# Four-layer image network on one core: the last image's activations kept in SBUF, its offset work split by halves, and two rules of the instruction planner changed

## The chip, the core and the metric

One NeuronCore of a Trainium2 chip runs the whole program in one launch. Its engines are TensorE (PE, with weight loads as PEld), VectorE (DVE), ScalarE (ACT), GpSimd (POOL) and the DMA queues, of which SyncE (SP) issues most. The metric is the device time of the launch in microseconds; lower is better. Every number below is from one core.

## What is computed

Four images of 96 channels by 64 x 64 pixels (`B, C, H, W = 4, 96, 64, 64`, so `L = 4096` positions) pass through four residual layers. All numbers are float32 except inside the two feed-forward parts, which round to 8 and 16 bits.

```python
x = x + L0(group_norm(x))            # a selective scan in four directions
x = x + L1(group_norm(x))            # a deformable 3x3 convolution
t = tokens(x)                        # L tokens of 96 channels
t = t + fourier(layer_norm(t))       # 192 hidden channels, DFT along the tokens and back
t = t + ffn2(layer_norm(t))
t = t + linear_attention(layer_norm(t))
t = t + ffn3(layer_norm(t))
```

Layer 0 projects each pixel to 192 channels, convolves, and then runs `h = exp(d*A)*h + d*u*B` over the 4096 positions, for 192 channels with 16 states each, along rows, columns, and both reversed; the four results are summed, normed over channels, gated by `z` and projected back to 96 channels. Layer 1 computes from the normed image 18 offsets and 9 masks per pixel by a 3x3 convolution, fetches for each of the 9 taps four neighbouring pixels at the shifted place, weighs them bilinearly, and multiplies by a 96 x 96 matrix per tap. The rest works on tokens.

## The kernel before

The Python code writes instructions in one order per engine, and each engine runs its own list in that order, waiting on semaphores. What stands where in those lists is settled when the program is built, by a small planner.

**The scan is the backbone.** `Layer0.scan` (L900) makes 1536 units: per image 4 directions, 4 time steps of 1024 positions, 3 groups of 64 channels, 8 units each. A unit is a decay on ACT (L1016), two products on PE that spread `d*u` (L1022), a product on DVE (L1036), the scan itself on DVE (L1044), a product on POOL (L1053) and sums on PE (L1072). Its tiles come from the pool `l0s`: twelve buffers of tag `da` (128 x 1024) and two of tag `bc` (128 x 2 x 1024). ACT's queue issues the `da` loads, SP's the others.

**Two streams fill in beside it.** `ends()` makes the inputs of the scan for images 0 to 3 (`first`, `before`) and then runs layers 2 and 3 of images 0, 1, 2, 3 one after the other (`Layers23.image`). `middle()` runs for each image `Layer0.behind` (sum of directions, norm, gate, projection: `x1`, L1094) and `Layer1.image` (L1223: `offsets`, `positions`, `sample`: `x2`). A stream is a generator that yields, after each few instructions, a `Step` with the time that they are taken to need on each engine. `Clock` adds these up. `pipe` (L272) keeps several chains of one kind open at once and picks the first whose tokens (`takes`, `frees`) and PSUM banks are free and that `Clock.has_room` lets in. `Stream.step` does the same for a stream. `has_bank` (L403) limits the PSUM banks that chains hold over a step to three; after the scan the stream `ends` gets five banks of its own.

**Who goes first.** After each scan unit `go()` lets every stream place one step, `middle` ahead of `ends`; from the moment the last image is being sampled, `ends` is asked first. After the scan the function `alone()` does the same without units.

**Layer 1 of an image.** `offsets` (L1242) loads `x1` from DRAM, takes the group norm's statistics (`bn_stats`, L448), norms `x` in place on ACT (L1262) and copies it with POOL into a padded tile (L1264). Then eight chunks of 512 positions follow: the 3x3 convolution on PE (L1280), its bias on ACT (L1291), four transposes of pixels (L1297), a copy to `pix` (L1299), the fold of the four partial sums (L1302), and eight DMAs per chunk that write the pixels four times into the gather table in DRAM (L1312, 64 in all). `positions` (L1317) loads the constant `base` and computes on DVE, for all 32 blocks of 128 pixels at once, the index and the four weights of each tap. Its tiles lie where those of `offsets` lay. `sample` (L1368) has 32 blocks x 3 chains: three indirect DMAs from POOL (L1385), the weighing, transposes on PE (L1418), and for each pair of blocks nine products with the weights (L1434), after which `x1` is loaded from DRAM, added (L1439), and stored as `x2` (L1441). During the scan ACT does the weighing (L1397), after it DVE (L1404 to L1406).

**Layers 2 and 3 of an image.** `Layers23.image` waits until `x2` of the image is complete, loads it (L1827), norms all of it (`normed`, L1605), and runs the Fourier part in two halves of channels: `hidden` (L1553), first DFT (L1512), twiddle (L1578), inverse (L1512), last (L1592, L1597). For the last image the rest is done in two halves of tokens side by side.

Of the kernel before, what the change touches and what calls it, by code (L numbers as in the profile page):

```python
# [8 lines left out]
F32 = mybir.dt.float32  # L9
# [11 lines left out]
L = H * W  # L21
# [250 lines left out]
def pipe(net, chains, width, every=0, lane=None, **tiles):  # L272
# [5 lines left out]
    while True:  # L278
# [9 lines left out]
        for n, chain in enumerate(active):  # L288
            if chain.new and not net.has_bank():
                continue  # L290
# [6 lines left out]
            if not all(free[tag] > 0 for tag in chain.takes):  # L297
                continue
# [5 lines left out]
        for tag in chain.takes:  # L304
            free[tag] -= 1
# [54 lines left out]
class Net:  # L360
# [3 lines left out]
    def __init__(self, ctx, tc, ins):  # L364
# [20 lines left out]
        self.sampling_last = False  # L385
        self.clock, self.known, self.streams, self.stream = Clock(), {}, [], None
# [16 lines left out]
    def has_bank(self):  # L403
        if self.own_banks:
            return self.stream.held < (5 if self.stream.own else 3)
        return sum(stream.held for stream in self.streams) < 3
# [36 lines left out]
    def group_norm_stats(self, x, pool, key, stats):  # L443

        nc = self.nc
        st = pool.tile([C, NCH, 6], F32, name=f"gnst{key}", tag="gnst")
        for j in range(NCH):
            nc.vector.bn_stats(st[:, j, :], x[:, j * CH : (j + 1) * CH])  # L448
            if j % 2:
                yield cost(dve=1.4)  # L450
# [22 lines left out]
    def centred(self, x, cen, dst, key, pool, bias=None, groups=(0, 1)):  # L473
# [7 lines left out]
        def chain(j):  # L481
            yield wait(new=True, takes="sq")
# [72 lines left out]
class Layer0:  # L555
# [440 lines left out]

    def fetch_step(self, u):

        u.bc = self.sp.tile([128, 2, T], F32, name=f"bc{u.key}", tag="bc")
        for s in range(2):  # L1000
            src = self.bc_d[u.b][u.k][NS * s : NS * s + NS, u.ts]
            self.net.nc.sync.dma_start(u.bc[:, s, :], src.unsqueeze(1).to_broadcast([NS, D8, T]))
# [91 lines left out]
    def behind(self, b):  # L1094
# [6 lines left out]
        with (  # L1101
# [3 lines left out]
            cen_a, cen_c, wo_a, wo_c = (net.load(q, big) for q in ("cen_a", "cen_c", "wo_a", "wo_c"))  # L1105
            for j0 in range(NCH - HB, -1, -HB):
                if j0 % (NCH // 2) == NCH // 2 - HB:

                    h0 = H // 2 * (j0 * 2 // NCH)
                    yta = big.tile([128, W, H // 2], F32, name=f"yta{b}_{h0}", tag="yta")  # L1110
                    ytc = big.tile([D2, W, H // 2], F32, name=f"ytc{b}_{h0}", tag="ytc")
                    for yt, c0 in ((yta, 0), (ytc, 128)):
                        src = self.y_d[b][3][c0 : c0 + yt.shape[0]].rearrange("c (w h) -> c w h", h=H)
                        nc.sync.dma_start(yt, src[:, :, h0 : h0 + H // 2])
                    yta_v, ytc_v = (t.rearrange("p w h -> p h w") for t in (yta, ytc))
                    yield wait(4.0)
                while not all((b, 2, j * CH // T) in self.summed for j in range(j0, j0 + HB)):
                    yield BLOCKED
                ca = big.tile([128, HB, CH], F32, name=f"ca{b}_{j0}", tag="ca")
# [5 lines left out]
                def centred(i):  # L1125
# [8 lines left out]
                    for y, yt in ((ya, yta_v), (yc, ytc_v)):  # L1134
                        y = y.rearrange("p (h w) -> p h w", w=W)
                        nc.gpsimd.tensor_add(y, y, yt[:, rs, :])
                    yield cost(pool=3.1, new=True)
# [22 lines left out]
                nw = op.tile([128, CH], F32, name=f"nw{b}_{j0}", tag="nw", bufs=1)  # L1160
# [3 lines left out]
                def gated(i):  # L1164
# [16 lines left out]
                    for o, n, z, vg, vb in parts:  # L1181
                        nc.gpsimd.tensor_mul(o[:, i, :], o[:, i, :], z)
                    xr = op.tile([C, CH], F32, name=f"xr{b}_{j}", tag="xr")
                    nc.sync.dma_start(xr, ins["x"][b][:, cs])
                    yield cost(pool=2.6, new=True)
# [6 lines left out]
                    yield cost(dve=0.7)  # L1192
                    nc.sync.dma_start(self.x1[b][:, cs], xr)
                    yield NOTHING

                yield from pipe(self.net, (gated(i) for i in range(HB)), 2)


class Layer1:
# [23 lines left out]
    def image(self, b):  # L1223
        tc = self.net.tc
        with tc.tile_pool(name=f"l1i{b}", bufs=1, side="right") as ix:
            idx = ix.tile([128, 288], U32, name=f"idx{b}", tag="idx")
            wt = ix.tile([128, 288, 4], F32, name=f"wt{b}", tag="wt")
            yield from self.before(b, idx, wt)
            self.net.sampling_last = b == B - 1
            yield from self.sample(b, idx, wt)  # L1230
        self.net.sampled.add(b)

    def before(self, b, idx, wt):
# [3 lines left out]
        with tc.tile_pool(name=f"l1o{b}", bufs=1, side="right") as keep:  # L1237
            om = keep.tile([128, 32, 27], F32, name=f"om{b}", tag="om")
            yield from self.offsets(b, om)
            yield from self.positions(b, om, idx, wt)  # L1240

    def offsets(self, b, om):  # L1242

        net = self.net
        tc, nc = net.tc, net.nc
        with tc.tile_pool(name=f"l1a{b}", bufs=1, side="right") as pre:
            x = pre.tile([C, L], F32, name=f"x1_{b}", tag="x")
            nc.sync.dma_start(x, self.x1[b])
# [4 lines left out]
            yield wait(4.0)  # L1253
            stats = []
            yield from net.group_norm_stats(x, pre, f"1_{b}", stats)
# [3 lines left out]
            yield cost(dve=0.2)  # L1259
            def filled(j):  # L1260
                cs = slice(j * CH, (j + 1) * CH)
                nc.scalar.activation(x[:, cs], x[:, cs], AF.Identity, scale=rstd, bias=nmr)  # L1262
                yield cost(act=0.8)
                nc.gpsimd.tensor_copy(  # L1264
                    pad[:, 1 + j * NR : 1 + (j + 1) * NR, 1 : 1 + W],
                    x[:, cs].rearrange("p (h w) -> p h w", w=W),
# [676 lines left out]
```

## Time and profile before

| what | value |
|---|---|
| median of 3 runs | 8444.11 us (8442.93 to 8499.31) |
| the profiled execution's own time | 8460.68 us |
| its span, first to last instruction | 8458.9 us |
| busy: PE, DVE, POOL, ACT | 76%, 80%, 66%, 59% of the span |
| first and last scan on DVE start at | 189.2 us, 7407.8 us |
| DMA | 1608.26 MB, 190 GB/s over the span |
| mean granted PE clock | 0.793 of full |

The profile is of one execution, 16.6 us above the median of the runs; the span is the time from the first to the last instruction. The page divides the span into 40 slices of 211 us and gives each engine's busy share in tenths. "Granted clock" is the share of full speed that PE's clock had. An answer by windows gives, for each stretch, its length, then the busy time and the number of instructions of each engine, then the granted clock, the DMA engines' share and what they moved in GB/s. The chain of waits follows the work that ended last back to what released it. fp32 products show as two rows of the profile for one instruction of the program. The table below puts names to the stretches after the last scan.

| us from the start | what ends each stretch |
|---|---|
| 7411 to 7472 | `x1` of the last image complete |
| 7472 to 7523 | first product of its offset convolution |
| 7523 to 7578 | last write of its gather table |
| 7578 to 7607 | first transposes of gathered pixels |
| 7607 to 8041 | last chunk of `x2` |
| 8041 to 8082 | first product of its Fourier part |
| 8082 to 8459 | end |

### The profile page before, as it was taken

What the parts mean: (1) busy time and instruction counts of PE and PEld (TensorE: products, weight loads), DVE (VectorE), ACT (ScalarE), POOL (GpSimd) and SP (SyncE); (2) the same over time, 40 slices, a digit from 0 to 9 for tenths busy, and PEclk for the clock granted to TensorE, in tenths of its full rate; (3) what the DMA queues carried; (4) which work ended last, traced back from release to release, by engine and by line L of the source; (5) the groups of instructions that cost most, each with busy time, mean ns of one, the idle gap of its engine ahead of it and who ended that gap; (6) DMA issues with size and microseconds to landing.
All of it is one profiled execution on the core that took longest, in us unless ns stands there. A gap on an engine that the chain in (4) does not pass through costs nothing.

```text
span 8458.9 us, 96090 instructions
## 1 busy us (share of the span) xinstructions
PE 6423.3 (76%) x31810; PEld 2788.5 (33%) x31848; DVE 6748.3 (80%) x5122; ACT 5005.0 (59%) x9171; POOL 5580.3 (66%) x4308
## 2 busy tenths in 40 slices
PE   6776777679767776877667788877688867788687
PEld 2211221112222233321122366422265522365373
DVE  2699989987688998778899889798988889827714
ACT  5665566646467787755577666454566775423224
POOL 0466556665468888756588888676788887617700
PEclk9776786778667777977778788877789878888798
DMA  3687778977678998877789899876899988745420
GB/s 92 162 217 200 170 190 223 227 177 188 152 210 233 236 244 224 214 168 190 201 236 246 224 236 235 195 177 165 218 236 232 235 206 192 169 103 159 145 61 16
DMA packets 773925, 1608.26 MB, mean 190 GB/s; under 512 B 264081, under 2 KB 355757, under 8 KB 771222
## 3 DMA queue, kind: packets, MB, share of 16 engines
q10 hardware_dynamic: 244224, 843.17, 39.7%
q1 hardware_dynamic: 455478, 532.37, 24.2%
q0 software_dynamic: 73728, 226.57, 10.1%
q8 instruction: 256, 4.19, 0.2%
q14 instruction: 239, 1.96, 0.1%
HBM read 1345.43 MB, written 256.29 MB: 189 GB/s over the span
## 4 chain that ended last, share of the span: by engine, by line
PE 32%; DVE 28%; DMA 11%; POOL 10%; ACT 9%; issue 8%; ACTq 1%; SPq 1%; DVEq 0%; another core or an unknown queue 0%; POOLq 0%
DVE da L1044 13%; POOL da L1053 7%; DVE db L1036 7%; PE pc L763 4%; PE ps L1418 3%; PE py L1072 3%; PE f L1512 3%; ACT g L1397 2%; PE pd L1434 2%; PE db L1022 2%; ACT da L1016 2%; POOL g L1385 2%; DMA da<-de 1%; DMA du<-du 1%; PE h L1553 1%
## 5 line engine op out<-in xcount | busy, mean ns | idle before, releaser
L1053 POOL TENSOR_TENSOR da<-da,bc 128x1024 f32<-128x1024 f32 x1536 | 3636.1, 2369 | 286.4 <-DVE da L1044 166.4
L1044 DVE TENSOR_TENSOR_SCAN da<-da,st,db 128x1024 f32<-128x1024 f32 x1152 | 2700.6, 2344 | 115.6 <-ACT da L1016 5.2
L1036 DVE TENSOR_TENSOR db<-db,bc 128x1024 f32<-128x1024 f32 x1536 | 1865.6, 1215 | 647.8 <-PE db L1022 646.2
L1016 ACT ACTIVATE da<-da,w_al 128x1024 f32<-128x1024 f32 x1536 | 1739.4, 1146 | 384.0 <-DMA da<-de 148.3
L1385 POOL DMA_INDIRECT g<-table,idx x1152 | 1199.8, 1042 | 378.2 <-issue 177.0
L1022 PE MATMUL db<-du,rep 24*128 24x512 bf16 x3072 | 690.5, 454 | 804.0 <-DVE da L1044 763.7
L1072 PE MATMUL py<-da,w_fold 128*32 128x512 f32 x6144 | 1076.7, 774 | 24.0 <-POOL da L1053 11.8
L1397 ACT ACTIVATE g<-g,wt 128x96 f32<-128x96 f32 x3456 | 969.4, 365 | 80.9 <-PE py L1072 19.8
L1044 DVE TENSOR_TENSOR_SCAN da<-da,db 128x1024 f32<-128x1024 f32 x384 | 877.2, 2284 | 58.0 <-ACT da L1016 21.9
L1418 PE MATMUL ps<-w_ident,g 128*96 128x128 f32 x3744 | 678.6, 331 | 205.0 <-issue 51.1
L1022 PEld LDWEIGHTS <-rep 24*128 24x128 bf16 x3072 | 148.6, 93 | 1929.7 <-DVE da L1044 1188.0
L850 POOL TENSOR_TENSOR lw<-lw,w 128x512 f32<-128x512 f32 x192 | 244.1, 1271 | 678.1 <-DVE w L848 634.8
L1051 POOL COPY st<-da 128x1 f32<-128x1 f32 x1152 | 228.7, 199 | 696.0 <-DVE da L1044 666.2
L1418 PEld LDWEIGHTS ps<-w_ident,g 128*96 128x96 f32 x3744 | 502.1, 149 | 532.0 <-ACT g L1397 151.2
L763 PE MATMUL pc<-pad,wc 96*128 96x512 f32 x1152 | 579.2, 640 | 13.5 <-DMA wc<-wc_d 4.1
L1426 ACT COPY st<-ps 96x384 f32<-96x384 f32 x384 | 180.4, 473 | 530.4 <-PE ps L1418 483.4
L884 PE MATMUL pr<-ex,w_ident 128*128 128x512 f32 x384 | 295.4, 861 | 71.0 <-DVE ex L864 19.4
L840 PE MATMUL pd<-xd,w_dtw 103*64 103x512 f32 (+1 forms) x512 | 270.1, 798 | 81.6 <-DMA w_dtw<-in_dtw 29.7
L763 PEld LDWEIGHTS pc<-pad,wc 96*128 96x128 f32 x1152 | 218.3, 200 | 313.1 <-issue 284.5
L1434 PE MATMUL pd<-st,wdc 96*128 96x256 f32 x1152 | 313.2, 421 | 3.2 <-ACT zt L789 1.8
L886 ACT CAST du<-pr 128x512 bf16<-128x512 f32 x192 | 111.6, 581 | 275.2 <-PE pr L885 190.1
L1521 ACT COPY d<-f 128x512 f32<-128x512 f32 x192 | 111.6, 583 | 273.3 <-PE f L1512 272.9
(260 smaller groups left out, 8860.8 us busy)
## 6 DMA issues: line engine op xcount, KB each, us to landing
da<-de ACTq DMA_DIRECT2D x1536, 512.0 KB
du<-du SPq DMA_DIRECT2D x1536, 96.0 KB
bc<-bcd SPq DMA_DIRECT2D x128, 512.0 KB
y<-yb SPq DMA_DIRECT2D x384, 128.0 KB
de<-rl SPq DMA_DIRECT2D x128, 256.0 KB
m<-in_dft SPq DMA_DIRECT2D x128, 256.0 KB
ad<-y ACTq DMA_DIRECT2D x192, 128.0 KB
table<-pix SPq DMA_DIRECT2D x256, 96.0 KB
```

The costliest lines, as they stand in the source:

```text
L763: nc.tensor.matmul(pp, lhsT=wc[:, q, g * 128 : (g + 1) * 128], rhs=pad[:, r0 + dy : r0 + dy + NR, dx : dx + W], start=(q == 0), stop=(q == 8),
L884: nc.tensor.matmul(pr, lhsT=net.ident, rhs=ex, start=True, stop=False)
L1016: self.net.nc.scalar.activation(u.da, u.da, AF.Exp, scale=self.al[:, a : a + 1])
L1022: self.net.nc.tensor.matmul(db[:, h, :], lhsT=self.rep[64 * u.q + 32 * h : 64 * u.q + 32 * h + 24], rhs=u.du[64 * u.q + 32 * h : 64 * u.q ...
L1036: self.net.nc.vector.tensor_mul(u.db, u.db, u.bc[:, 0, :])
L1044: nc.vector.tensor_tensor_scan(u.along(u.hh), u.along(u.da), u.along(u.db), first, ALU.mult, ALU.add)
L1053: self.net.nc.gpsimd.tensor_mul(u.hh, u.hh, u.bc[:, 1, :])
L1072: nc.tensor.matmul(py[p0 : p0 + 32], lhsT=self.fold[:, u.i, :], rhs=hc[:, h * CH : (h + 1) * CH], start=u.sums["add"] is None and u.i == 0 ...
L1385: nc.gpsimd.indirect_dma_start(out=g[:, k, :], out_offset=None, in_=self.tables[b % 2], in_offset=bass.IndirectOffsetOnAxis(ap=idx[:, n : ...
L1397: nc.scalar.activation(pixel, pixel, AF.Identity, scale=wt[:, n, c : c + 1])
L1418: nc.tensor.matmul(pt[:, k, :], lhsT=g[:, k, c * C : (c + 1) * C], rhs=net.ident, is_transpose=True, start=(c == 0), stop=(c == corners - 1),)
L1434: nc.tensor.matmul(po, lhsT=wdc[:, k, :], rhs=st[:, k, :], start=(k == 0), stop=(k == 8))
```

## The change

For the last image (`b == B - 1`) only:

- `x1` is a tile in SBUF. `behind` loads the image's input into it whole, adds to it chunk by chunk, and takes `bn_stats` of each chunk at once. `yta` and `ytc` come in quarters and not halves. In its final pair of chunks the sums of directions and the gate run on DVE, not POOL.
- `sample` adds into the same tile, so that it becomes `x2`; the stores and loads of both fall away. Work tiles come from the scan's `da` and `bc` buffers (`ring`, `wide`). Two `st` and two `xo` may be open at once.
- `positions` runs for 16 blocks at a time: the first half after four chunks of the convolution, the second as the first chain of `sample`.
- the first norm of layers 2 and 3 runs in two halves; each chunk waits only for its own part of `x2` (`net.arrived`).
- after the scan, until the last image is being sampled, `ends` gets a turn only when `middle` can place nothing.

For every image:

- `offsets` norms straight into the padded tile (the copy on POOL falls away) and writes the whole gather table first, in four parts of 1024 positions: 8 DMAs each, twice as large, 32 in all. For images 0 to 2 `pix` has one buffer of twice the size instead of two, for the last four. The transposes become products of 64 pixels with the unit matrix.
- in `pipe`, a chain that is not the front one may take a PSUM bank only if another stays free, unless the front chain holds one already.

```diff
-            if chain.new and not net.has_bank():
+            if chain.new and not net.has_bank(1 + (n > 0 and not active[0].holds)):
                 continue
...
-    def has_bank(self):
+    def has_bank(self, n=1):
         if self.own_banks:
-            return self.stream.held < (5 if self.stream.own else 3)
-        return sum(stream.held for stream in self.streams) < 3
+            return self.stream.held + n <= (5 if self.stream.own else 3)
+        return sum(stream.held for stream in self.streams) + n <= 3
...
+    def ring(self, name, n, dtype=F32):
+
+        return self.sp.tile([128, T], dtype, name=name, tag="da", bufs=12)[:, :n]
+
+    def wide(self, name):
+        return self.sp.tile([128, 2, T], F32, name=name, tag="bc").rearrange("p s t -> p (s t)")
...
-                        nc.gpsimd.tensor_add(y, y, yt[:, rs, :])
+                        (nc.vector if ends else nc.gpsimd).tensor_add(y, y, yt[:, rs, :])
...
                     nc.vector.tensor_add(xr, po[:C], xr)
-                    yield cost(dve=0.7)
-                    nc.sync.dma_start(self.x1[b][:, cs], xr)
-                    yield NOTHING
+                    if x1 is None:
+                        yield cost(dve=0.7)
+                        nc.sync.dma_start(self.x1[b][:, cs], xr)
+                        yield NOTHING
+                    else:
+                        nc.vector.bn_stats(st[:, j, :], xr)
+                        yield cost(dve=1.4)
...
+            def table(jj):
+
+                yield wait(new=True, takes="pix")
+                if place_of is None:
+                    pix = pre.tile([128, 8, C], F32, name=f"pix{b}_{jj}", tag="pix")
+                else:
+                    pix = l0.ring(f"pix{b}_{jj}", 8 * C).rearrange("p (q c) -> p q c", c=C)
+                for h in range(2):
+                    pt = net.mm(f"pt{b}_{jj}_{h}")[:, : 4 * C].rearrange("p (q c) -> p q c", c=C)
+                    for q in range(4):
+                        for r in range(2):
+                            row = pad[:, 1 + 16 * jj + 8 * h + 2 * q + r, 1 : 1 + W]
+                            nc.tensor.matmul(
+                                pt[64 * r : 64 * r + 64, q, :],
+                                lhsT=row,
+                                rhs=net.ident[:C, :C],
+                                start=True,
+                                stop=True,
+                            )
+                    nc.scalar.copy(pix[:, 4 * h : 4 * h + 4, :], pt)
+                    yield cost(pe=0.9, act=0.5, new=h == 0)
+                for q in range(4):
+                    dy, dx = divmod(q, 2)
+                    for r in range(2):
+                        y0 = 2 + 16 * jj + r - dy
+                        dst = v[y0 : y0 + 15 : 2, 2 - dx : 2 - dx + W, q * C : (q + 1) * C]
+                        nc.sync.dma_start(dst.rearrange("t w d -> w t d"), pix[64 * r : 64 * r + 64])
+                yield wait(frees="pix")
...
+            def chains():
+                for jj in range(NCH // 2):
+                    yield table(jj)
+                for j in range(NCH):
+                    yield chunk(j)
+                    if place_of is not None and j == 3:
+                        yield place_of(0)
...
-                nc.sync.dma_start(self.x2[b][:, cs], xo)
+                if not last:
+                    nc.sync.dma_start(self.x2[b][:, cs], xo)
+                elif j % 2:
+                    net.arrived[f"x{j // 2}"] = 1
...
+                if b == B - 1:
+                    for r in range(2):
+                        yield from normed(net, t, tl, f"2_{b}_{r}", pool, (r,), True)
+                else:
+                    yield from normed(net, t, tl, f"2_{b}", pool)
...
+            if clock.own is not None and not net.sampling_last:
+                return any(stream.step() for stream in streams[::-1])
             return any([stream.step() for stream in (streams if net.sampling_last else streams[::-1])])
```

## The prediction

> **What bounds the kernel now.** I read the page's slices first, then the stretches after the last scan, then the chain of waits through them, then a stop of the scan.
>
> ```profile
> PE   6776777679767776877667788877688867788687
> ...
> DVE  2699989987688998778899889798988889827714
> ```
>
> Up to slice 35 (35 x 211.5 = 7402 us) DVE carries the scan and is busy eight to nine tenths of the time. From slice 36 on it is not, and PE does most. So two parts must be costed apart: 7411 us with the scan, and a tail of 8459 - 7411 = 1048 us, in which only image 2's end and image 3 are left.
>
> ```profile
> core 0: us, PE busy (x) PEld busy (x) DVE busy (x) ACT busy (x) POOL busy (x), PEclk, DMA share, GB/s
> ...
> 7411.00:7472.00 61.00, 54.56 (x444) 39.38 (x444) 5.72 (x9) 21.56 (x40) 13.26 (x13) 0.92 0.35 97
> 7472.00:7523.00 51.00, 45.41 (x302) 35.64 (x304) 16.16 (x24) 13.94 (x24) 4.91 (x8) 0.63 0.27 74
> 7523.00:7578.00 55.00, 52.25 (x480) 33.51 (x469) 6.41 (x13) 11.21 (x25) 0.00 (x0) 0.97 0.60 116
> 7578.00:7607.00 29.00, 21.11 (x334) 20.83 (x335) 14.89 (x26) 8.06 (x12) 10.60 (x10) 0.77 0.39 122
> 7607.00:8041.00 434.00, 322.05 (x1663) 208.43 (x1661) 330.48 (x464) 131.63 (x267) 334.31 (x280) 0.80 0.51 150
> 8041.00:8082.00 41.00, 24.90 (x56) 9.21 (x58) 7.57 (x12) 10.20 (x19) 0.00 (x0) 0.75 0.18 42
> 8082.00:8459.00 377.00, 324.16 (x2948) 236.18 (x2946) 127.34 (x218) 125.73 (x237) 7.19 (x2) 0.90 0.12 39
> ```
>
> The first four rows, 196 us, bring image 3 from the last scan to the first transposes of its samples. PE is busy 173 of them, and most of that is image 2's Fourier part: by line, 24.8 us inverse DFT, 21.2 last, 20.9 hidden, 18.2 twiddle, 14.9 output, 11.0 first DFT. The 434 us of sampling are POOL's: 288 gathers, 1.5 us apart, and still 1.38 us apart (29 in 40 us) after 7990 us, when image 2 is done. The 41 us are `x2` to DRAM and back and one norm.
>
> ```profile
> 7470.96 9.50 DMA x<-x
> 7480.57 4.85 DVE gnst L448 x8
> 7487.52 5.22 PE yp L1592 x32
> ...
> 7513.43 5.07 PE yp L1592 x32
> 7518.50 3.52 PE o L1597 x4
> 7522.02 7.50 PE po L1280 x36
> ...
> 7575.31 2.31 DMA table<-pix
> ...
> 8041.26 1.67 DMA x<-xo
> 8043.03 8.98 DMA t<-x
> ```
>
> Image 3's chain waits 9.5 us for `x1` to come back, then its first convolution product (L1280) stands in PE's list behind 35 us of image 2 (7487 to 7522).
>
> **The tail up to the first transposes.** The built order of the changed program shows what stands in PE's list. Because `ends` arrives earlier (image 2's norm at scan unit 1487, not 1511), image 2's first inverse DFT and first twiddle are placed before the last scan: 24.8 + 18.2 = 43 us of PE leave these 196 us. The other Fourier work stays: at the first transposes image 2 stands at the same product in both programs. So giving the chain the first turn reorders and moves no more than that. The 64 products with the unit matrix have no row; the nearest is hidden (97 x 64 by 97 x 96, 20.9 us for 128), so 64 cost 10.4 us against 4.4 for the transposes that they replace: +6. PE's sum is 173 - 43 + 6 = 136 us.
>
> [...] PE's clock is 0.50 from 7490 to 7525, all 35 us, though PE is busy throughout; before it PE was idle for the `x1` load and the statistics. [...] by the row, half of 35, 17 us. [...] but the changed chain has shorter idle times of its own (3 us waiting for `ya`, 2 at the gate)[...]. I take 10[...]: 126 us. Idle of PE was 23 us; in the changed order it has other work ready at the `x1` and norm steps, and I leave 14: the two waits, some PSUM waits, and the second half of the positions (16 small DVE operations at half of the present rows' 9.4 us), which stand in DVE's list ahead of the first weighing. That makes 140 us, first transposes at 7551: **56 us saved**, between 40 and 70.
>
> The other things on this path are inside it: adds on DVE at 0.67 us (L1175, same shape) for 1.51 on POOL (four, 3.4 us), gates 0.67 for 1.27 (four, 2.4), `x1` store and load (9.5), half of the statistics already taken. PE's list is longer than that chain. The table: its last issue now comes at 7575, 43 us after its first. [...] The rows give 142 GB/s at a DMA share of 0.7 while 64 issues of 0.62 us take 40 us. By issue alone, 32 DMAs would take 20 us; [...] 6.3 MB need still 32 (at share 1.0) to 43. I take 43. It begins when PE has passed image 2's last, output and hidden parts (57 us), the end of `x1` (20) and 9 of the first DFT, about 7411 + 86: gathers start near 7541, not 7594. So POOL starts 53 us earlier, in step with PE.
>
> **Sampling** keeps its 434 us. Same gathers; the order of PE around them is the same through image 2; the 32 small DMAs that go were hidden (DMA share 0.51). Most of image 3's norm (up to 25 us of PE, by the row of the 41 us) moves in here; it would cost if PE were full, but image 2 is done by then and PE busy for 20 of 40 us.
>
> **After the last sample.** 10.7 us of store and load go. Of the norm only the last chunk is left: add 0.5, product 1.1, two ACT passes 1.2, four sums 2.4, three ACT passes 2.0, three DVE 1.9, four spreads and a product 5.7: 15 us for 41. **26 us saved.** The 377 us stay.
>
> **The scan part, 7411 us.** Up to scan unit 325 the orders are the same but for one swapped product. Then:
>
> ```profile
> 2355.62 6.39 SPq L1312 DMA_DIRECT2D table<-pix  x8
> 2363.89 1.28 ACT L1332 ACT_TABLE_LOAD   x1 [16.78 <-DMA table<-pix]
> 2367.31 0.76 DVE L1336 TENSOR_TENSOR pos<-om,w_base 128x576 f32<-128x576 f32 x1 [20.80 <-DMA de<-rl]
> ```
>
> For image 0 the positions' tiles lie where `pix` lay, and the load of `base` is queued on SP behind the last table writes: DVE, with the scan behind it, stands 20.8 us. For image 1 it stands 11.5, for image 2 not. In the changed order the table is written 18 units earlier and no write precedes `base`: I leave 3.5 us of landing each, and gain 25. Against it: `pix` for images 0 to 2 now has one buffer, so three copies per image wait on ACT for eight writes (6 us of issue plus landing), with decays and `da` loads queued behind them. The copies stand 1 to 3 units (4.7 us each) apart. The old waits of this kind (16.2 us, 7 times) cost little; nine waits cost 0 if ACT's lead of two units absorbs them, 9 x 9.4 = 85 if each is lost whole; nearer to the old row: 10. The Fourier work that moves in: 24 more units at 43 per 200 us (5200 to 5600) rather than 47: 10. Four statistics on DVE, 2.7. Net: -25 + 10 + 10 + 3 = -2. The bank rule reshuffles 1200 units; that can be worth 40 either way, and no row prices it.
>
> **Sum.** 56 + 26 + 2 = 84 us. On the profiled span, 8459 - 84 = 8375. That execution (8460.7) lies 16.6 above the median, so for the median 8444 - 84 = **8360**.
>
> **Rivals.** (1) *The chain gains little:* image 2's products still stand in front of it in PE's list, the clock still drops, and the table's 43 us start late. Then PE's 43 us that left are given back in part: 25 + 26 = 51 saved, less 10 for the scan: 8403. For it: the same place of image 2 at the first transposes. Against it: a sum of PE that is smaller by 37 us whatever the clock does. (2) *The reserved bank smooths the scan:* DVE waited 646 us for PE's spread (L1036). If a chain that finds no bank no longer blocks PE's list, a tenth of this, 65 us, comes on top: 8295. For it: `ends` is 24 units ahead. Against it: most of these waits are the loop PE waits for DVE, 764 us. (3) *Slower:* the single `pix` buffer stalls ACT, decays and `da` loads come late, and the scan stops at each of nine copies. From 84 / 9 = 9.3 us lost per copy it eats all gains; at 15 us, 135 are lost: 8495. Against it: the copies are spread over 5 to 9 units, and the writes of a part need about 10 us.
>
> **How the numbers follow.** Forecast 0.47 (8330 to 8385), rival 1 0.25, rival 2 0.22, rival 3 0.06. The range leaves out rival 3 and the edge of 2: 8300 to 8425. One per cent, about what can be told from no change here, is 84 us: the forecast stands on the line. Half of it (0.24) and all of rival 2 and a little more give 0.48 for faster by over 1%; 0.46 for within; 0.06 for slower.
>
> **What would show it.** Right: first transposes about 140 us after the last scan, clock no longer 0.50 for 35 us there; first gather near 130 us after it; 434 us of sampling; hidden 15 us after the last sample; no 20 us wait at the positions of image 0; last scan within 40 us of 7408. Wrong: ACT waiting for table writes at the `pix` copies for over 9 us each; gathers slower than 1.5 us; image 2 unfinished when sampling ends.

## The result, and the profile after

| kernel | median of its runs | beside it, the kernel before | ratio, 95% interval |
|---|---|---|---|
| changed | 8372.06 us (8358.2 to 8389.31) | 8451.97 us | 0.9895 [0.9853, 0.9938] |
| changed, run again | 8330.55 us (8303.98 to 8370.54) | 8438.84 us | 0.9874 [0.9842, 0.9907] |

The change makes the kernel 1.1 to 1.3% faster; 8360 was predicted. The profiled execution of the changed kernel took 8389.31 us (span 8387.5), the longest of its first four. The page's slices:

```profile
PE   6776777779767778877767888776888787887787
...
DVE  2799889987799988777898888998887988846724
```

The shape is that of before: DVE carries the scan up to slice 35, PE the rest. The last scan starts at 7373.9 us, 7407.8 before. The stretches after it, in the columns of the earlier answer:

```profile
7376.00:7431.00 55.00, 52.64 (x346) 29.62 (x346) 25.54 (x33) 17.00 (x29) 3.21 (x2) 0.96 0.32 82
7431.00:7460.00 29.00, 28.34 (x390) 27.95 (x391) 10.96 (x25) 8.77 (x15) 0.61 (x4) 0.90 0.02 6
7460.00:7498.00 38.00, 38.00 (x367) 19.83 (x366) 5.24 (x16) 13.56 (x26) 0.32 (x1) 0.96 0.78 207
7498.00:7531.00 33.00, 17.68 (x216) 15.65 (x214) 7.30 (x18) 7.33 (x12) 16.81 (x18) 0.69 0.37 108
7531.00:7994.00 463.00, 337.41 (x1621) 213.72 (x1622) 335.24 (x472) 139.51 (x282) 320.21 (x272) 0.78 0.43 130
7994.00:8009.00 15.00, 9.55 (x21) 3.03 (x20) 5.08 (x8) 3.01 (x5) 0.00 (x0) 0.77 0.00 0
8009.00:8387.00 378.00, 323.44 (x2952) 236.63 (x2952) 127.33 (x218) 125.70 (x237) 7.45 (x2) 0.90 0.12 39
```

The rows end at: `x1` complete (7431), first product for the table (7460), first gather (7498), first transposes of gathered pixels (7531), last chunk of `x2` (7994), first Fourier product (8009), end. From the scan to the first transposes it is 155 us (196 before), and 15 us from the last sample to the Fourier part (41 before); the sampling itself takes 463 us (434 before). So this profile's tail is only 37 us shorter. Its chain of waits:

```profile
7380.21 7.16 PE f L1635 x112
7387.37 1.04 PE py L1083 x8
7389.09 2.25 DMA y<-yb
...
7431.06 7.66 PE h L1680 x96
...
7450.90 9.29 PE f L1635 x144
7460.18 5.28 PE pt L1358 x128
```

The scan's last sum (`py`) is queued behind 112 rows (56 products) of image 2's inverse DFT, so the last `y` leaves 13 us after the scan. The 9.5 us for `x1` to DRAM and back are gone. But from 7431 to 7460, with `x1` complete, the chain still passes through 29 us of image 2 (`h`, `f`) before the table's products (`pt`) get their turn.

What made the sampling longer is seen when the same program is profiled a second time (the second row of the first table). The two answers on what POOL waited for, the first profile and then the second, have columns of total us, times, longest:

```profile
POOL g L1495 <- PE ps L1528: 55.6, 18, 12.4
```

```profile
POOL g L1495 <- PE ps L1528: 12.4, 11, 7.8
```

```profile
7391.00:7512.00 121.00, 118.06 (x1086) 76.71 (x1086) 41.48 (x73) 38.98 (x70) 3.50 (x6) 0.94 0.39 103
7512.00:7527.00 15.00, 14.67 (x226) 14.43 (x224) 7.67 (x19) 7.45 (x12) 11.61 (x11) 1.00 0.46 134
7527.00:7966.00 439.00, 329.88 (x1622) 210.05 (x1622) 335.68 (x471) 139.01 (x282) 333.23 (x279) 0.80 0.48 141
7966.00:7980.00 14.00, 8.53 (x23) 2.91 (x23) 5.08 (x8) 3.01 (x5) 0.00 (x0) 0.88 0.01 1
```

In the second profile the gathers wait 43 us less for transposes. There the stages are 136 us (121 + 15) to the first transposes, 439 of sampling and 14 after it; the span is 8357.6 us. The last section comes back to the difference.

### The profile page after: what moved, and what is told of

It is laid out like the page before. It is cut to its first block, busy times and chain, and to the rows that moved or that the text cites. A ratio compares the mean times of both kernels' runs of the same rounds, so it can differ in the third digit from the quotient of the medians.

```text
span 8387.5 us, 96574 instructions
## 1 busy us (share of the span) xinstructions
PE 6457.2 (77%) x32232; PEld 2791.3 (33%) x32232; DVE 6737.2 (80%) x5149; ACT 5007.3 (60%) x9177; POOL 5539.7 (66%) x4268
## 3 DMA queue, kind: packets, MB, share of 16 engines
q0 software_dynamic: 73728, 226.57, 10.2%
## 4 chain that ended last, share of the span: by engine, by line
PE 31%; DVE 27%; DMA 11%; POOL 11%; ACT 9%; issue 8%; SPq 2%; ACTq 1%; DVEq 0%; another core or an unknown queue 0%; POOLq 0%
DVE da L1055 13%; POOL da L1064 7%; DVE db L1047 6%; PE pc L767 4%; PE f L1635 3%; PE py L1083 3%; PE ps L1528 3%; ACT g L1507 2%; POOL g L1495 2%; DMA da<-de 2%; ACT da L1027 2%; PE db L1033 2%; PE pd L1547 2%; DMA du<-du 2%; DMA m<-in_dft 1%
## 5 line engine op out<-in xcount | busy, mean ns | idle before, releaser
L1083 PE MATMUL py<-da,w_fold 128*32 128x512 f32 x6144 | 1103.2, 787 | 26.5 <-POOL da L1064 11.0
```

The source lines that it names most:

```text
L1083: nc.tensor.matmul(py[p0 : p0 + 32], lhsT=self.fold[:, u.i, :], rhs=hc[:, h * CH : (h + 1) * CH], start=u.sums["add"] is None and u.i == 0 ...
```

## The experiments

The stages of the profiles side by side, in us: start of the last scan plus 2.3 (its end), from there to the first gather, from the first gather to the last `x2` chunk, from there to the first Fourier product of image 3. "Unit" is the scan unit at which image 2's first norm stands in DVE's list (1536: after the scan).

| kernel | ratio to before | unit | scan ends | to 1st gather | sampling | to Fourier |
|---|---|---|---|---|---|---|
| before | 1 | 1511 | 7410 | 184 | 447 | 41 |
| changed, 1st / 2nd profile | 0.9895 / 0.9874 | 1487 | 7376 / 7391 | 122 / 122 | 497 / 454 | 15 / 14 |
| changed without the bank rule | 1.0045 | 1536 | 7454 | 134 | 453 | 78 |
| bank rule alone | 0.9958 | 1498 | 7380 | 170 | 487 | 38 |
| rule only for layers 0 and 1 | 0.9969 | 1509 | 7438 | 124 | 530 | 20 |
| last image alone | 0.9949 | 1509 | 7429 | 120 | 494 | 33 |

The last stretch, to the end, takes 377 to 381 us in all. The experiments come from four sessions, in which the kernel before took 8439, 8498, 8485 and 8484 us; each ratio is taken within its session, but stages of profiles from two sessions can differ by as much. A difference in us worked out from two ratios has an error of some 15 to 30 us. Scan ends of single profiles scatter: eight profiles whose scan lists are those of the changed kernel, or differ from them only at its `pix` copies or its end, lie between 7335 and 7416, at 7383 in the mean.

### The changed kernel again

> The changed kernel itself, once more, as the yardstick for the runs beside it. Expected: ratio to the kernel before 0.990 +- 0.003; last scan starts near 7374 us, first transposes near 155 us after the end of the last scan. Both theories expect the same here; how far the stages differ from those of the first profile tells how small a difference a single profile can show.

Measured: 0.9874 [0.9842, 0.9907], last scan at 7388.5 us, first transposes 137 us after the scan. The scan came within 15 us; the tail is 45 us shorter than in the first profile, nearly all of it in the sampling. Scan and sampling of a single profile scatter by as much. The stretch to the first gather (122 both times) and the one after the last sample (15 and 14) repeat, and differences of 5 us or more in these two are read below.

### Without the rule on banks

```diff
-            if chain.new and not net.has_bank(1 + (n > 0 and not active[0].holds)):
+            if chain.new and not net.has_bank():
```

> The changed kernel with the rule on PSUM banks in the planner undone. My theory: the 34 us by which the last scan starts earlier come from the two stops of DVE at the positions of images 0 and 1 (32.3 us before, 0 now), so the last scan still starts at 7374 +- 15 us and the ratio to the kernel before stays 0.988 to 0.993. Rival: the rule keeps TensorE's list moving and made the gain in the scan; then the last scan starts at 7395 us or later and the ratio is 0.994 or more.

Measured: 1.0045 [1.0025, 1.0064]. My theory fell at once, and the prediction's view of the rule with it. The rival's two marks (7395 us or later, 0.994 or more) are passed. All other parts of the change, without one line of the planner, make the kernel slower than before; the line is worth 1.0045 - 0.9874 = 1.7%, some 144 us of 8440. The stops at the positions are as absent as in the changed kernel (1.6 us in all), so they are not what the rule brings. Two things are lost. The scan ends 63 us later than in the second profile, 71 later than the mean of eight, and image 2 is so late that image 3 has to wait for it:

```profile
7454.00:7588.00 134.00, 127.65 (x1079) 74.12 (x1078) 37.20 (x74) 44.94 (x80) 4.20 (x7) 0.91 0.31 78
7588.00:8041.00 453.00, 379.49 (x2833) 285.08 (x2834) 328.75 (x445) 141.53 (x284) 343.49 (x289) 0.88 0.51 152
8041.00:8118.00 77.00, 54.07 (x112) 17.59 (x110) 39.20 (x78) 28.62 (x54) 3.51 (x1) 0.71 0.06 21
```

The chain up to the first gather costs only 12 us more. The sampling absorbs more of image 2 (PE busy 379 us instead of 330) at the same length. But image 2's output leaves only at 8080 us, 39 us after the last sample, and 77 us pass before image 3's first Fourier product.

### The rule alone, and the rule in one stream

The rule put into the kernel before is the last diff the other way round, with the new `has_bank(n)`. The rule kept for the stream of layers 0 and 1 alone, in the changed kernel:

```diff
-            if chain.new and not net.has_bank(1 + (n > 0 and not active[0].holds)):
+            if chain.new and not net.has_bank(1 + (n > 0 and not active[0].holds and not net.stream.own)):
```

> The kernel before with nothing but the new rule on PSUM banks. My theory by now: what counts is how far the stream of layers 2 and 3 has come when the scan ends, told by the scan unit at which image 2's first norm stands in DVE's list: 1511 before, 1487 in the changed kernel, 1536 (after the scan) in it without the rule. Between the last two lie 153 us for 49 units, 3.1 us a unit. Here it stands at 1498, 13 units earlier than before: 40 us less, ratio 0.995. Rival: the rule takes its time out of the scan itself, by fewer stops of TensorE's list, whatever else is in the program; then it brings here what it brought there, 150 us, ratio 0.982.

> The changed kernel with the rule on banks kept only for the stream that makes layers 0 and 1, and undone for layers 2 and 3. Image 2's first norm then stands at scan unit 1509 (1487 with the whole rule, 1536 without). My theory: 22 units x 3.1 us = 68 us longer than the changed kernel, ratio to before 0.995 to 0.997. Rival: only stops within the scan count and these come from the stream of layers 0 and 1 with its four open chains; then this run is like the changed kernel, 0.988.

Measured: 0.9958 [0.9941, 0.9975] and 0.9969 [0.9953, 0.9986]. Both rivals are out of their intervals; 3.1 us for each scan unit by which image 2 starts later gave both numbers ahead of the runs. The rule is thus worth 35 us to the kernel before and 144 to the rest of the change. In the scan most of this goes through the wait that the second rival of the prediction named, DVE's wait for PE's spread of `d*u`. The stretch from 200 to 7330 us of the second profile of the changed kernel, then of the one without the rule, each with this wait in it (us, times, longest):

```profile
200.00:7330.00 7130.00, 5456.79 (x25638) 2158.34 (x25636) 6132.79 (x4264) 4564.22 (x8401) 5144.66 (x3937) 0.78 0.82 208
DVE db L1047 <- PE db L1033: 627.3, 291, 19.8
```

```profile
200.00:7330.00 7130.00, 5382.05 (x24731) 2120.04 (x24729) 6074.26 (x4200) 4498.09 (x8282) 5086.46 (x3899) 0.78 0.81 206
DVE db L1047 <- PE db L1033: 667.9, 298, 16.5
```

Without the rule DVE does 59 us less in the same time, and 41 us of that are this wait. Over the whole scan it is 708 us without the rule, and 612 to 668, 645 in the mean, in the eight profiles of the changed kernel's lists. In the kernel before the rule takes 36 us off it, by a pair of single profiles, whose scatter is as large:

```profile
DVE db L1036 <- PE db L1022: 611.7, 317, 18.0
```

```profile
DVE db L1036 <- PE db L1022: 575.6, 283, 15.9
```

Between the kernel before and the changed one this cannot be seen (646 us, then 644 and 668), because the new tables lengthen the same wait: it is 630 us with the last image alone, the next run, and 708 when the tables come in without the rule. Counted while the lists are built, up to the end of the scan: the front chain of a `pipe` is refused a bank 185 times without the rule and 119 times with it, chains behind it 543 and 1710 times. That fits a front chain that is held up less; that this is what shortens the wait is argued, not shown.

### The last image alone

The rule undone, and images 0 to 2 by the old `offsets`:

```diff
-                    yield from self.offsets(b, None, None, om, None, l0)
+                    yield from self.offsets_old(b, om)
```

> Only the changes to the last image: the rule on banks is undone, and images 0 to 2 norm, convolve and write their tables by the code of before. The lists of the scan part are then those of before (image 2's first norm at unit 1509, 1511 before). The prediction's two tail terms, 56 us up to the first transposes and 26 us after the last sample, should then be here whole if they belong to the last image's chain: 82 us, ratio 0.990. Rival, from the runs so far: the 43 us of TensorE that left the tail came from the rule, which brings image 2 forward; with image 2 as late as before, the chain still stands behind it, and at 3.1 us a unit from 1487 the total is 68 us above the changed kernel's, ratio 0.995.

Measured: 0.9949 [0.9926, 0.9971], about 43 us. The forecast of 82 is outside the interval, the rival's number inside, but the rival's reason is wrong too: the first gather comes 120 us after the scan, as early as in the changed kernel, with image 2 as late as before.

```profile
7429.00:7548.00 119.00, 108.87 (x969) 73.26 (x969) 25.60 (x47) 45.70 (x84) 2.74 (x5) 0.96 0.46 131
7548.00:8042.00 494.00, 374.46 (x2301) 254.15 (x2301) 351.30 (x504) 141.67 (x285) 339.36 (x289) 0.79 0.44 131
8042.00:8075.00 33.00, 24.40 (x50) 8.64 (x48) 9.24 (x15) 11.97 (x22) 3.51 (x1) 0.79 0.02 7
```

In these 119 us PE still runs image 2's whole first inverse DFT and twiddle:

```profile
L1710 PE MATMUL f<-w_idft,d 128*64 128x64 f32 x384 | 24.9, 289 | 0.6 <-ACT d L1781 0.6
L1780 PE MATMUL zp<-d,m 128*128 128x96 f32 x128 | 19.3, 316 | 5.6 <-DMA m<-in_dft 5.3 <-ACT yb L1094 0.2
```

What stood in front of the chain before and does not now is the later work of image 2. It has moved behind the chain, into the sampling (374 us of PE instead of 330). It ends there: image 2's output leaves 5 us before the last sample, and the 33 us after it are 19 more than in the changed kernel. In sums (a ratio's distance from 1, times 8440 us): last image alone -43 us, with the new tables of images 0 to 2 added +38, with the rule added to both -106. So without the rule the new tables cost 81 us (here with an error of some 25), and the rule is what makes them bearable. The rule and the last image with the old tables were not run together.

### The turn after the scan, and the norm by halves

```diff
-            if clock.own is not None and not net.sampling_last:
-                return any(stream.step() for stream in streams[::-1])
```

> The changed kernel without the first turn for the last image's chain after the scan (both streams are asked again). As the prediction had it, the turn only reorders: image 2 stands at about the same product when the first gathered pixels are transposed, so the first transposes stay within 15 us of 155 us after the last scan and the total within 0.2%. Rival: the turn is what shortens the tail; then this stage is 30 us longer or more and the ratio to the kernel before is 0.993 or more.

Measured: 0.9880 [0.9851, 0.9909], first gather 134 us after the scan instead of 122, first transposes 147 us after it, inside the forecast. The turn brings the first gather 12 us forward, and the total shows none of it beyond its interval. The rival is out.

```diff
-                    for r in range(2):
-                        yield from normed(net, t, tl, f"2_{b}_{r}", pool, (r,), True)
+                    while b not in net.sampled:
+                        yield BLOCKED
+                    yield from normed(net, t, tl, f"2_{b}", pool)
```

> The changed kernel with the last image's first norm of the Fourier part taken whole, begun when all of x2 is there. Prediction's term: the 41 us after the last sample fell by 10.7 us of store and load and by 15 us of norm that moved in among the samples. Then this run shows about 30 us from the last sample to the first Fourier product (15 in the changed kernel), and the total is 15 us (0.2%) longer. Rival: the halves only move work to a place where it costs sampling as much; then the time from the last sample is 30 us but the sampling is shorter by some 10 us and the total is the same.

Measured: 26 us from the last sample to the first Fourier product instead of 14, so 12 to 13 us for the halves, 15 predicted; the sampling stays at 455 (454). The total, 0.9888 [0.9861, 0.9914], has risen by as much as expected, which is less than its interval can tell.

### Two small pix buffers for images 0 to 2

```diff
+                    if place_of is None:
+                        pix = pre.tile([128, 4, C], F32, name=f"pix{b}_{jj}_{h}", tag="pix", bufs=2)
...
+                    if place_of is None:
+                        writes(jj, pix, 2 * jj + h, 8)
```

> The changed kernel with two pix buffers of half the size for images 0 to 2, each written by eight half-size DMAs, as before the change; the last image as in the changed kernel. In four profiles of the changed order ACT stands 71 to 76 us at the pix copies of these images (nine waits of about 8 us), 11 us before the change. The prediction took 10 us for what this costs the scan, because ACT runs ahead of DVE. Then this run is 10 us (0.1%) shorter than the changed kernel, with the waits at 20 us or less. Rival (the prediction's third): each of these stops also stops the scan; then the scan part is 60 us or more shorter, ratio 0.981 or less.

Measured: 0.9875 [0.9836, 0.9913]: the total is that of the changed kernel, and the rival (0.981) is out. The waits did not go down to 20 us as I expected: they are 64, in the changed kernel 71 to 76. In the first profile of the changed kernel, before 7000 us, ACT stood idle at these copies until (us, times):

```profile
  DMA table<-pix: 40.0, 5
  DMA du<-du: 31.5, 4
```

Nine waits of 8 us, close to the 9.3 from which the prediction's third rival would have eaten all gains, and yet no loss that can be measured. But as the other buffers only moved the waits, this run bounds nothing more than their difference. A measure of what the stops pass on is DVE's wait for ACT's decays in the scan: 27 us before, 39 and 44 in the two profiles of the changed kernel, 24 in the one without the rule on banks. By this measure they pass on no more than 17 us, where the prediction took 10.

### Three other edits of the last image

The scan's last sums ahead of all steps:

```diff
-            while go():
+            while l0.next is not None and go():
```

> The changed kernel in which no step of the two streams is placed any more once the last scan unit is in the lists, until its sums are, so that TensorE's last sum is not queued behind 112 products of image 2's inverse DFT. In the changed kernel the last y store leaves 13 us after the last scan has begun to end, before the change 2 us after. Theory: the last image's chain starts 10 us earlier and, as it is first, keeps 5 to 10 us of them: first gather at 112 to 117 us after the scan and not 121. Rival: TensorE is the limit of this stage and stands idle while it waits for the sums; then the first gather stays at 121 us or comes later, and the total is the same.

Measured: first gather at 116 us, inside the forecast of 112 to 117; total 0.9876 [0.9837, 0.9915], the same. Six of the ten microseconds arrive at the gathers, and none can be seen at the end.

Both halves of the positions after the convolution:

```diff
-                yield wait(takes="g half" if last and t >= 16 else "g")
+                yield wait(takes=f"g half{t // 16}" if last else "g")
...
-                    yield place_of(1)
+                    yield place_of(0)
+                    yield place_of(1)
```

> The changed kernel with both halves of the last image's positions after all eight chunks of its convolution. Theory: the first gather, 121 us after the scan in the changed kernel, where it waits for the last convolution product, comes 9 to 15 us later, and as GpSimd sets the pace from there on, the total is 10 us longer (0.1%). Rival: TensorE is what the samples wait for at first, so nothing is lost. Where TensorE runs single products of the inverse DFT 1.4 us apart (seen in the first profile of the changed kernel while 16 gathers were issued, 7502 to 7523 us, not in the second): if the gathers cause it, it starts after the first gather here too; if it is the program's own, it is at the same products, ahead of the gathers.

Measured: first gather at 126 us, 4 us later and not 9 to 15: in the changed kernel it waits for the last convolution product (`po`) anyway, which ends 11 us after the index of the first half is there (7496.8 and 7485.4 us in the first profile). The total, 0.9916 [0.9884, 0.9948], is 0.3 to 0.4% above the changed kernel's, more than the 0.1% expected, with overlapping intervals; in its profile the gathers wait 75.9 us for transposes. What this run says on that is told in the last section.

The adds and gates of the last pair of chunks on GpSimd:

```diff
-                ends = b == B - 1 and j0 == 0
+                ends = False
```

> The changed kernel with the sums of directions and the gates of the last pair of chunks back on GpSimd. The prediction counted 3.4 and 2.4 us for these, inside TensorE's longer list. Theory: the first gather stays within 3 us of 121 us after the scan and the total is the same. Rival: the last image's chain, which now goes first, is what this stage waits for; then the first gather is 6 us later.

Measured: first gather at 117 us, 4 us earlier than in the changed kernel, one more than the forecast allowed, and not later; total 0.9882 [0.9843, 0.9922], the same. The 5.8 us lie inside PE's list, as the prediction had it.

### Layers 2 and 3 first

```diff
-            return any([stream.step() for stream in (streams if net.sampling_last else streams[::-1])])
+            return any([stream.step() for stream in streams])
```

> The changed kernel with the stream of layers 2 and 3 asked first after each scan unit, not only from the last image's sampling on. Image 1 is then finished 104 scan units earlier (1345 instead of 1449), but x2 of image 2 comes 13 units later, and image 2's first norm stands at unit 1496 instead of 1487. My theory: the start of image 2 is what counts; 9 units x 3.1 us = 28 us longer than the changed kernel, ratio to before 0.991. Rival: the sum of the work of that stream done by the end of the scan counts wherever it lies, so that the stretch of the scan after unit 1345, with less work beside it, runs faster; then the scan ends 20 us or more earlier and the ratio is 0.985 or less.

Measured: 1.0078 [1.0052, 1.0105]. Both theories miss by far: 28 us were expected, it is some 170 more than the changed kernel, and more than 100 of them are in the scan, which ends at 7497 us. So 3.1 us a unit is a rule for programs with this order of turns and no law. From 200 to 7330 us PE is busy 5367 us and DVE 6026 (5457 and 6133 in the changed kernel's second profile): all of the program is late there, which does not tell why. DVE's wait for PE's spread is 685 us, 40 above the mean of the changed kernel's lists. Why serving that stream first slows the scan is open.

## Why the prediction was right, and where it was wrong

**The tail's terms: right in size.** Up to the first transposes 56 us less were predicted, 41 and 59 were measured (two profiles; 155 and 137 us against a forecast of 140). The first gather was put at 130 us after the scan and came at 122. After the last sample 26 less were predicted, 26 and 27 measured, and the run with the whole norm shows the share of the halves as 12 to 13 of the 15 in the sum. The sampling was to stay at 434: it is 439 in the second profile, 463 in the first. One term had the wrong size without effect: the products with the unit matrix were put at 10.4 us for 4.4, +6, and take 5.5.

**The reason given for the first term: wrong.** The step that failed is "43 us of PE leave these 196 us", taken as what shortens them. The run with the last image alone has image 2 as late as before, and its first gather is as early as the changed kernel's; without the rule, with nothing of image 2 done ahead, it loses 12 us. In the run with the last image alone the 43 us have not left: 24.9 us of inverse DFT and 19.3 of twiddle stand in the 119 us up to the first gather. What shortens this stretch is the last image's own part of the change, behind which other work of image 2 now queues. Of it the first turn is 12 us and the early positions 4; how the rest divides between `x1` in SBUF, the table written first and in half the DMAs, and the clock was not taken apart. The sentence that "giving the chain the first turn reorders and moves no more than that" held only because image 2 had come further; otherwise its work moves into the sampling, where PE took 44 to 50 us more of it, and what is more comes out behind the last sample (33 and 78 us instead of 14).

**The scan's terms: a wrong sum.** -2 us were predicted for the scan part, -34 and -19 measured in two profiles, about -27 against 7410 in the mean of eight. The stops at the positions were taken at -25, and all of the 32.3 us went: after the change DVE runs from a scan straight into image 0's positions, with no wait in front (the first instruction there takes 2.35 us, the two others like it 0.73).

```profile
2332.75 2.34 DVE L1055 TENSOR_TENSOR_SCAN da<-da,st,db 128x1024 f32<-128x1024 f32 x1
2335.00 2.35 DVE L1435 TENSOR_TENSOR pos<-om,w_base 128x576 f32<-128x576 f32 x1
```

The rule was passed over with "that can be worth 40 either way, and no row prices it". It was worth 35 us alone and 144 with the rest, and the new tables, of which only the stops at the positions (-25), ACT's waits (+10) and the statistics (+3) were counted, cost 81 us without it. (Of the seven old waits by which ACT's term was judged, 16.2 us, four with 9.6 us belong to the last image and lie after the scan.) Together the two bring 63 us where the sum had 2, and the last image alone brought 43 of its 82. These misses have opposite signs, so the number came out right in part by luck. A row of the profile does move with the rule, DVE's wait for PE's spread, but its size could not tell beforehand how much; the built lists could have warned: the prediction read 1487 in place of 1511 there and did not ask which edit had moved it.

**The clock.** Up to the first gather the granted clock is 0.90 to 0.96 in the rows of the first profile and 0.94 over all 121 us of the second; the 35 us at 0.50 are gone, as expected. The 10 us taken for it were the author's estimate and were not measured apart. In PE's work the difference is larger: image 2's `yp` (128 rows, L1592) and `o` (16 rows, L1597) took 21.2 and 14.9 us between the last scan and the first transposes of before, and the same numbers of rows 11.8 and 8.5 us between the last scan and the first gather of the changed kernel's first profile, 16 us less.

**The table's writes.** 43 us were taken, from the 142 GB/s of the rows before. SP issued the 64 writes of before without a pause, and now the 32:

```profile
7530.54 45.39 SPq L1312 DMA_DIRECT2D table<-pix  x64
```

```profile
7462.71 25.60 SPq L1372 DMA_DIRECT2D table<-pix  x32
```

From 7463 to 7488 us the rate is 230 GB/s at a DMA share of 0.89, with pieces of 384 bytes as before. So the 142 GB/s of the rows before go with the 64 issues in 45 us and not with the size of the pieces: the estimate by issue alone, 20 us, was the nearer to the 25.6. The first gather waits for a convolution product and no longer for the table.

**The rivals.** The first (the chain gains little) is out: 122 us to the first gather. The second was right that the rule matters and, within the scan, on where: with the rest of the change the rule takes 40 us or more off DVE's wait for PE's spread (63 against the mean of eight profiles; the rival said 65). Its total of 8295 was not reached, because the new tables put as much on the same wait (630 us with the last image alone, 708 with them and without the rule). The third named a real wait (nine of 8 us), of which no more than 17 us are seen to reach DVE. That the program without one line would end on the slower side was in none of them.

## What to carry to other kernels

When a planner makes the lists, price its edits one at a time on the built lists before summing the others: the position of the stream that fills in the gaps, at the end of the stage that bounds, told here within 0.2% what a line of the planner was worth, as long as the order of turns stayed. Work that a chain overtakes is not gone; look for where it comes out, and whether the engine has room there. A time that agrees with the forecast does not confirm its terms: only taking the parts out one by one showed two that were missing.

## What the runs showed of the hardware

In the first profile PE runs image 2's products singly or a few at a time, about 1.4 us apart, while the first 18 gathers are issued 1.25 us apart; a row alone takes 0.3 us.

```profile
7513.22 0.27 PE L1635 MATMUL f<-w_dft,d 128*64 128x64 f32 x1 [1.13 <-issue]
7514.64 0.36 PE L1635 MATMUL f<-w_dft,d 128*64 128x64 f32 x1 [1.16 <-issue]
...
7523.05 7.22 PE L1635 MATMUL f<-w_dft,d 128*64 128x64 f32 x112 [0.44 <-issue]
```

"Issue" says that nothing in the profile explains the wait. It begins 5 us after the first gather (7497.7 us) and ends 3 us after the last of the burst was issued (7520); then 112 rows take 7.2 us. With the positions late, the gathers come at other products, and the slow stretch moves with them: first gather at 7492.7 us, slow from 7497.4 to 7519.5, last of the burst at 7514.0. In these two profiles it goes with the gathers (it begins 5.2 and 4.7 us after the first of them) and not with a place in the program.

The DMA queues of the kind "instruction" (q8 and q14, 0.2% and 0.1% of the 16 engines' time over the first profile) show no delay there: in the first profile none of their packets lies between 7502 and 7524 us, the long run of products starts before the next one (7524.8 us), and the 16 KB packets on either side took 1.2 to 1.4 us. Between 7000 and 8500 us the 62 packets of q8 took 0.3% of the engines' time in both profiles, some 1.0 to 1.3 us each. The second profile of the same program has the same burst with 160 rows in one run of 10.2 us beside it, so the burst alone does not make the stretch.

Of fourteen profiles the gathers' waits for transposes are 5 to 12 us in five and 40 to 79 in nine. The kernel does not tell the two kinds apart (the kernel before is among the five, the same with the rule alone among the nine), the session does: all four profiles of the session of the second profile are among the five, all eight of the three other sessions among the nine. The chip does not, as one chip has both kinds. The kernel before is 45 to 59 us faster in that session, so that it may have the stretch in the others too, and the ratios, taken within a session, need not contain it: the changed kernel has 0.9874 there, the runs with other `pix` buffers and with the sums first 0.9875 and 0.9876 elsewhere. What differs between the sessions is open. The stretch cost the first profile 43 us, more than most parts of the change are worth: a sampling time is to be read with this wait beside it.
